# A transposing DMA in place of sixteen TensorE transposes in the feed-forwards that run beside attention

## The chip, the cores and the metric

The kernel runs on one core of one Trainium2 chip. The metric is the device time of one execution in microseconds (us); lower is better. Before the change the median of three runs is 2065.4 us (2061.41, 2065.40 and 2065.89). A forecast within 0.2% of the time before cannot be told from no change.

## What is computed

Four sequences (B = 4) of 512 tokens with 512 features pass through two layers, each with an attention part and a feed-forward part, all as residual updates scaled by the tanh of a gate:

```python
x = x + tanh(g_xattn[0]) * L0_xattn(ctx_512, layernorm(x))   # top-k adjacency, 153 of 512 kept
x = x + tanh(g_ffn[0])   * L0_ffn(layernorm(x))              # Hadamard, 8-bit, ternary weights
x = x + tanh(g_xattn[1]) * L1_xattn(layernorm(x), ctx_512)   # 16 heads, rotary, softmax
x = x + tanh(g_ffn[1])   * L1_ffn(layernorm(x))              # 8-bit, ternary weights
```

Both feed-forwards have the same inner shape. A row of 512 features goes up to 2048 by two products with ternary weights, silu(gate) times up gives the inner layer, and that layer is quantized before the product down to 512:

```python
def act_quant(x):
    scale = 127 / max(max(abs(x), axis=-1), 1e-5)
    return clip(round(x * scale), -128, 127) / scale
out = act_quant(inner) @ weight_quant(w_down).T        # inner: (tokens, 2048)
```

In layer 0 a Hadamard transform of length 2048 stands between the inner layer and act_quant. The rounded inner layer holds whole numbers, so it is kept in bfloat16 exactly.

## The kernel before

One core does everything. Tokens are cut into tiles of 128 rows on 128 partitions; a sequence has four (NT = 4). The work runs in three stretches:

- Opening, about the first 260 us: adjacency of sequence 0, ternary weights of layer 0, and feed0 of sequence 0 by itself. Here the flag alone[0] is True.
- The attention of layer 1 (generator attention, L877): 4 sequences times 8 pairs of heads. Between its steps the background is woven in: adjacency and feed0 of sequences 1 to 3, then the ternary weights of layer 1 (last_weights), then feed1 of sequences 0 to 2. A table of jobs (L985) with a cost and a due step decides how many background steps go between two attention steps. The flag is False here (L959).
- Close: feed1 of sequence 3 (L1015 on). The flag is True for that tile's own steps and False for what is left of feed1 of sequence 2, which is woven in (L1016 to L1020).

The order in which the source issues steps is only a first order. A scheduler in the compiler places every instruction in a fixed queue of its engine, by priorities and by its own estimates, and tile pools with fixed numbers of buffers decide what has to wait. Each engine, and the DMA queue of SyncE (SP), then takes its queue strictly in order: an instruction that waits holds up all behind it.

The quantized product down is in projected (L362). For one tile of 128 tokens:

1. DVE takes the row maximum (L377), scales and rounds with a magic number (L382), and unmagic (L205) writes q, 128 x 2048 bfloat16, on DVE (L210) when the flag is False, on ACT (L208) otherwise. q comes from a pool tag with one buffer.
2. turned (L197) turns q into zT, which has 16 blocks of 128 x 128: for each of four groups, four TensorE transposes into one PSUM bank (L202) and one ScalarE copy to SBUF (L203). zT has one buffer as well.
3. TensorE multiplies the 16 blocks with the ternary weights into pd (L399), with each block of zT as the loaded weight.
4. DVE adds pd to the residual (L569 in layer 0, L640 in layer 1).

The same helper turned is called with n = 1 for the 512 features at the entrance of each feed-forward (L541, L623), and with n = 4 for the inner layer (L393).

Background PSUM banks for turned come from bg_tr (L78): when the flag is False always from the background ring of two banks (tag bg), which it shares with the up and down products.

SP issues nearly all loads in one queue: the head weights wq (L731), wc (L734), wr (L736), the output weights om (L744) and the rotated keys kr (L800) of each pair, the raw weights of layer 1 (L222), the results (L642) and the spilled residuals (L581, L912). wc, wr and kr have one buffer and wq and om two, so most of these loads wait in SP's queue for TensorE to finish with the earlier contents.

Of the kernel before, what the change touches and what calls it, by code (L numbers as in the profile page):

```python
# [2 lines left out]

# [23 lines left out]
EPS = 1e-5  # L27
MAGIC = 12582912.0
GONE = -3.0e38
F8 = mybir.dt.float8e4  # L30


@with_exitstack
def flamingo_kernel(
# [9 lines left out]
    nc = tc.nc  # L44
# [20 lines left out]
    alone = [True]  # L65
# [12 lines left out]
    def bg_tr(name, dt=F32):  # L78
        if mine("tr", 4):
            return psb.tile([P, 4, P], dt, tag="bg", name=name)  # L80
        return pst.tile([P, 4, P], dt, tag="tr", name=name)
# [114 lines left out]

    def turned(src, dst, n, name):  # L197

        for k in range(n):
            pt = bg_tr(f"ptq_{name}_{k}", BF)  # L200
            for c in range(4):
                nc.tensor.transpose(pt[:, c, :], src[:, (4 * k + c) * P : (4 * k + c + 1) * P], identb)  # L202
            nc.scalar.copy(dst[:, 4 * k : 4 * k + 4, :], pt)  # L203
# [50 lines left out]
    def feed_weights(first, name):  # L254

        wa = bp.tile([P, NC, 2 * FF], F8, tag="wa", name=f"wa_{name}")
        wd = bp.tile([P, NF, D], F8, tag="wd", name=f"wd_{name}")
        down = (downT if first else outT).rearrange("(t c p) o -> t p c o", p=P, c=4)
# [103 lines left out]
    def projected(u, z, mul, wd, gd, last):  # L362
# [23 lines left out]
        else:  # L386
# [4 lines left out]
            yield 1.6  # L391
        zT = bp.tile([P, NF, P], BF, tag="zT", name=f"zT_{u}")
        turned(q, zT, 4, f"h{u}")  # L393
        col = small.tile([P, 1], F32, tag="cols", name=f"col_{u}")
        nc.vector.tensor_scalar(col, m, 1.0 / 127.0, gd, ALU.mult, ALU.mult)
# [14 lines left out]
    def adjacency(b):  # L410
# [16 lines left out]
        for two in range(0, NT, 2):  # L427
# [17 lines left out]
            for r in range(rounds):  # L445
# [5 lines left out]
                with tc.high_priority(offset=-FILL):  # L451
                    if r < rounds - 1:
                        for j in pair:
                            nc.vector.match_replace(works[j], m8[j], cur[j], GONE)  # L454
                            cur[j] = works[j]
# [44 lines left out]
    def feed0(b, w):  # L500
# [6 lines left out]
        for j in range(NT):  # L507
# [31 lines left out]
            unmagic(q, h)  # L539
            zq = bp.tile([P, NC, P], BF, tag="zq", name=f"zq_{u}", bufs=4)  # L540
            turned(q, zq, 1, f"a{u}")  # L541
            ready.append((zq, dg, du))
            yield 2.0
# [31 lines left out]
    def feed1(b, w, wn):  # L575
# [24 lines left out]
        for j in range(NT):  # L600
            u = f"g{b}_{j}"
            n = front_t(f"n_{u}")
            if quick:
                nc.scalar.activation(
                    n, xr[j], AF.Identity, bias=cc[:, j : j + 1], scale=ca[:, j : j + 1]
                )
                nc.vector.tensor_tensor(n, n, wn, ALU.mult)
            else:
                ln_tile(n, xr[j], j, mv, r)

                nc.vector.scalar_tensor_tensor(xr[j], n, tgf1, xr[j], ALU.mult, ALU.add)
                nc.vector.scalar_tensor_tensor(n, n, rr[:, j : j + 1], wn, ALU.mult, ALU.mult)
            amax = small.tile([P, 1], F32, tag="amax", name=f"amaxg_{u}")
            nc.vector.tensor_reduce(amax, n, AX.X, ALU.max, apply_absolute_value=True)
            yield 2.7
            m, sc = scales(amax, 1.0, f"g{u}")
            du = small.tile([P, 1], F32, tag="du", name=f"du_{u}", bufs=6)
            nc.vector.tensor_scalar(du, m, 1.0 / 127.0, s_gv, ALU.mult, ALU.mult)
            nc.vector.tensor_scalar(n, n, sc, MAGIC, ALU.mult, ALU.add)
            q = bp.tile([P, D], BF, tag="qa", name=f"qa_{u}")  # L620
            unmagic(q, n)
            zq = bp.tile([P, NC, P], BF, tag="zq", name=f"zq_{u}", bufs=4)
            turned(q, zq, 1, f"g{u}")  # L623
            ready.append((zq, du, du))
            yield 1.8
# [513 lines left out]
```

## Time and profile before

The profile is of one execution that took 2064.35 us, with 2062.6 us from its first to its last instruction.

| | busy us | share of the span | instructions |
|---|---|---|---|
| TensorE matmul (PE) | 1853.7 | 90% | 7274 |
| TensorE weight load (PEld) | 873.3 | 42% | 7274 |
| VectorE (DVE) | 1584.7 | 77% | 3233 |
| ScalarE (ACT) | 1176.6 | 57% | 1979 |
| GpSimd (POOL) | 333.1 | 16% | 316 |

The mean granted TensorE clock is 0.962 of full speed; the DMA engines moved 139.25 MB. Matmuls are pipelined, so the busy time of one is longer than the distance to the next: the distance is what the next matmul in the queue pays. In the profile's rows the letter f stands for feed0 and g for feed1, ptq for the PSUM tile of a transpose, and the number behind the tile is dropped. "idle before" is the time in which the engine stood still just ahead of the rows of the group.

### The profile page before, as it was taken

How to read it: one execution, taken by the hardware profiler on the slowest of the kernel's cores; microseconds unless marked ns; L12 is line 12 of the kernel's file. 1: busy time of each engine (PE TensorE's matmuls, PEld its weight loads, DVE VectorE, ACT ScalarE, POOL GpSimd, SP SyncE). 2: the span in 40 equal slices, each digit the busy share in tenths (PEclk: the TensorE clock that was granted, in tenths of full speed). 3: DMA queues.
4: the chain of work that ended last, by engine and by line, in shares of the span. 5: the costliest groups of instructions: out<-in, count | busy, mean ns of one | idle time of the engine just before them, and what ended most of it. 6: DMA issues, size and time to landing. Idle time of an engine off the chain costs nothing. (4 is left out here: it accounts for less than half of the span.)

```text
span 2062.6 us, 21752 instructions
## 1 busy us (share of the span) xinstructions
PE 1853.7 (90%) x7274; PEld 873.3 (42%) x7274; DVE 1584.7 (77%) x3233; ACT 1176.6 (57%) x1979; POOL 333.1 (16%) x316
## 2 busy tenths in 40 slices
PE   1268789999999999999999999999999999999898
PEld 0035434434544444445453444454444444444344
DVE  7989599986774999876769999767636755866775
ACT  6935454455544555455454554554899565567554
POOL 3010031122100221230011221300112210101000
PEclk6579899999999999999999999999999999999999
DMA  7451021210101222110012221101755111111000
GB/s 273 148 177 38 1 77 41 63 46 27 38 21 32 83 82 60 43 38 26 27 33 87 72 73 38 38 21 33 256 191 199 50 38 45 58 35 39 11 16 26
DMA packets 65633, 139.25 MB, mean 68 GB/s; under 512 B 7537, under 2 KB 18161, under 8 KB 62449
## 3 DMA queue, kind: packets, MB, share of 16 engines
q1 hardware_dynamic: 60048, 121.92, 18.7%
q0 software_dynamic: 4320, 14.16, 1.8%
q10 hardware_dynamic: 1152, 1.77, 0.2%
q8 instruction: 58, 0.95, 0.2%
q14 instruction: 55, 0.44, 0.1%
HBM read 117.90 MB, written 19.92 MB: 67 GB/s over the span
## 5 line engine op out<-in xcount | busy, mean ns | idle before, releaser
L793 POOL TENSOR_TENSOR ro<-ro,rs 128x512 f32<-128x512 f32 x192 | 252.7, 1319 | 1167.2 <-DVE rs L789 753.8
L834 ACT ACTIVATE pp<-pss,nm 128x512 f32<-128x512 f32 x256 | 175.1, 688 | 224.8 <-DVE nm L831 224.0
L764 PE MATMUL pqh<-hT,wq 128*128 128x512 f32 x512 | 239.6, 603 | 6.8 <-ACT pp L834 6.6
L853 PE MATMUL pc<-pT,kv 128*128 128x512 f32 x512 | 235.4, 598 | 0.7 <-ACT pT L846 0.6
L865 PE MATMUL po<-om,cxo 128*128 128x512 f32 x512 | 230.9, 597 | 0.0
L831 DVE TENSOR_REDUCE nm<-pss 128x1 f32<-128x512 f32 x256 | 167.6, 681 | 57.4 <-PE pss L826 56.5
L779 PE MATMUL pb<-qh,wc 128*128 128x512 f32 x384 | 191.1, 614 | 10.4 <-ACT qh L769 7.3
L449 DVE MAX8 m<-work 128x8 f32<-128x512 f32 x304 | 198.0, 680 | 0.6
L454 DVE MATCH_REPLACE8 work<-m,work 128x512 f32<-128x512 f32 x288 | 192.8, 674 | 0.1
L837 ACT ACTIVATE pp<-pp,rsm 128x512 f32<-128x512 f32 x256 | 178.9, 724 | 21.2 <-DVE rsm L836 20.9
L870 DVE SCALAR_TENSOR_TENSOR x<-po,gt,x 128x512 f32<-128x512 f32 x128 | 94.6, 744 | 92.4 <-PE po L865 91.9
L846 ACT COPY pT<-ppt 128x512 f32<-128x512 f32 x256 | 142.9, 592 | 28.9 <-PE ppt L845 28.8
L845 PEld LDWEIGHTS ppt<-ident,pp 128*128 128x128 f32 x1024 | 117.3, 141 | 86.0 <-issue 33.9
L845 PE MATMUL ppt<-ident,pp 128*128 128x128 f32 x1024 | 146.4, 277 | 6.7 <-ACT pT L846 3.5
L823 PE MATMUL pss<-kr,qr 64*128 64x512 f32 x256 | 144.3, 644 | 5.6 <-ACT pp L834 4.8
L764 PEld LDWEIGHTS pqh<-hT,wq 128*128 128x128 f32 x512 | 92.7, 191 | 125.4 <-issue 84.6
L826 PE MATMUL pss<-kr,qr 64*128 64x512 f32 x256 | 144.4, 645 | 0.5 <-DVE ro L787 0.5
L865 PEld LDWEIGHTS po<-om,cxo 128*128 128x128 f32 x512 | 93.7, 190 | 114.5 <-issue 98.1
L787 DVE TENSOR_TENSOR ro<-pb,cos_q 128x512 f32<-128x512 f32 x192 | 130.5, 680 | 11.0 <-PE pb L779 10.2
L853 PEld LDWEIGHTS pc<-pT,kv 128*128 128x128 f32 x512 | 92.7, 190 | 102.3 <-issue 88.7
L858 ACT COPY cxo<-pc 128x512 f32<-128x512 f32 x64 | 37.6, 587 | 135.7 <-PE pc L853 135.4
L750 PE MATMUL pr<-ro,wr 128*64 128x512 f32 x192 | 99.8, 613 | 14.3 <-POOL ro L793 12.2
(266 smaller groups left out, 3123.5 us busy)
## 6 DMA issues: line engine op xcount, KB each, us to landing
wq<-in_wqh SPq DMA_DIRECT2D x64, 256.0 KB, 2.7
om<-omd SPq DMA_DIRECT2D x64, 256.0 KB, 2.7
wc<-in_wkcq SPq DMA_DIRECT2D x32, 384.0 KB, 3.1
krd<-krs POOLq DMA_DIRECT2D x32, 256.0 KB, 2.4
kr<-krd SPq DMA_DIRECT2D x32, 256.0 KB, 2.7
sa_w1v<-in_gvT SPq DMA_DIRECT2D x8, 1024.0 KB, 5.3
sb_w1v<-in_gvT SPq DMA_DIRECT2D x8, 1024.0 KB, 5.5
wr<-in_wqr SPq DMA_DIRECT2D x32, 192.0 KB, 2.4
```

What stands on the lines that cost most here:

```text
L449: nc.vector.max(m8[j], cur[j])
L454: nc.vector.match_replace(works[j], m8[j], cur[j], GONE)
L764: nc.tensor.matmul(pq, self.wqs[i][:, c, :], hT[self.b][:, c, :], start=(c == 0), stop=(c == NC - 1),)
L779: nc.tensor.matmul(pb, self.wc[:, at : at + P], self.qhs[i if i < 2 else o], start=True, stop=True)
L793: nc.gpsimd.tensor_tensor(ro, ro, rs, ALU.add)
L826: nc.tensor.matmul(*args, start=True, stop=True)
L831: nc.vector.tensor_reduce(nm, pss[i], AX.X, ALU.max, negate=True)
L834: nc.scalar.activation(pp, pss[i], AF.Exp, bias=nm, accum_out=sm)
L837: nc.scalar.activation(pp, pp, AF.Copy, scale=rs)
L845: nc.tensor.transpose(pt[:, l, :], pp[:, l * P : (l + 1) * P], ident)
L853: nc.tensor.matmul(pc, kv[self.b][:, l, :], self.pT[i][:, l, :], start=(l == 0), stop=(l == NT - 1),)
L865: nc.tensor.matmul(po, self.cxo[i][:, j * P : (j + 1) * P], self.oms[i], start=(i == 0), stop=(i == 1),)
```

## The change

In turned, when n is above 1 and the flag is False, the loop of transposes and copies is not run; one transposing DMA is issued from SP, q to zT, and the function returns. Where the flag is True, and for n = 1, nothing changes.

```diff
-from contextlib import ExitStack
+from contextlib import ExitStack, nullcontext
...
+U16 = mybir.dt.uint16
 F8 = mybir.dt.float8e4
...
     def turned(src, dst, n, name):
 
+
+        if n > 1 and not alone[0]:
+            nc.sync.dma_start_transpose(dst, src)
+            return
         for k in range(n):
             pt = bg_tr(f"ptq_{name}_{k}", BF)
             for c in range(4):
```

The two new names at the top are not used. In the built kernel 24 transposing DMAs stand in SP's queue: four tiles each for sequences 1, 2 and 3 in feed0 and for sequences 0, 1 and 2 in feed1. TensorE's queue has 384 transposes fewer (of 7274 matmuls in the profile), and ScalarE's 96 copies fewer. The lines of the changed file lie five further down from this place on: the down product is L404, and the transposing DMA is L202.

## Prediction

> **What bounds the kernel now.** I read the page's busy rows first, then busy time by stage, because the change touches only the stretch with attention. The columns are length, then busy time of each engine with instruction counts, the granted TensorE clock, the DMA engines' share and GB/s.
>
> ```profile
> PE 1853.7 (90%) x7274; PEld 873.3 (42%) x7274; DVE 1584.7 (77%) x3233; ACT 1176.6 (57%) x1979; POOL 333.1 (16%) x316
> ```
> ```profile
> 520.00:940.00 420.00, 405.15 (x1537) 190.94 (x1536) 343.91 (x688) 215.00 (x410) 77.79 (x72) 0.99 0.16 49
> 940.00:1360.00 420.00, 404.75 (x1545) 189.92 (x1544) 345.03 (x693) 215.46 (x410) 79.76 (x72) 1.00 0.16 49
> 1360.00:1640.00 280.00, 265.72 (x1005) 124.60 (x1004) 177.16 (x332) 208.86 (x321) 45.04 (x33) 0.99 0.40 135
> ```
>
> TensorE is busy 96% of these stages at full clock, ACT about half, and the DMA engines 16%. TensorE time is what counts here, and it runs a fixed queue: an operand that comes late stops everything behind it. So I next looked at one tile's turn, in the timeline around 990 us (start, length, engine, line).
>
> ```profile
> 986.38 2.17 DVE L210 TENSOR_SCALAR q_f<-yb_f 128x2048 bf16<-128x2048 f32 x1
> ...
> 990.34 0.61 PE L202 MATMUL ptq_hf<-identb,q_f 128*128 128x128 bf16 x8
> ...
> 990.77 1.07 ACT L203 COPY zT_f<-ptq_hf 128x512 bf16<-128x512 bf16 x2 [1.52 <-PE ptq_hf L202]
> 990.79 1.08 PE L853 MATMUL pc<-pT,kv 128*128 128x512 f32 x2
> ...
> 991.70 0.61 PE L202 MATMUL ptq_hf<-identb,q_f 128*128 128x128 bf16 x8
> ...
> 993.07 3.62 PE L399 MATMUL pd_f<-wd_w,zT_f 128*128 128x512 fp8e4 x16
> ...
> 996.72 0.75 DVE L569 SCALAR_TENSOR_TENSOR x<-pd_f,col_f,x 128x512 f32<-128x512 f32 x1 [8.18 <-PE pd_f L399]
> ```
>
> Eight transposes take TensorE only from 990.34 to 990.79, 56 ns each, and lie among attention matmuls. pd starts 4.5 us after q ends at 988.55, with no gap. The last row says that DVE stands waiting for pd: a late pd is not absorbed there.
>
> **What it removes.** 24 tiles x 16 = 384 transposes. At 56 ns that is 21.5 us. The distances from each of them to the next matmul in the trace, added up, are 26.0 us, with a stall inside one group (3.1 us where others take 0.9). I take 25 us, all on the path, since TensorE is. It also removes 96 copies of 0.594 us, 57 us of ACT. ACT is not the bound, but in the waits of TensorE from 260 to 1960 us some 38 us end at ACT. A window of 420 us loses 16 copies or 9.5 us of its 215 us, 4.4%, which would be 1.7 us of those 38; since the copies stand close to other ACT work I take 3, between 0 and 10. Gain together: 28 us.
>
> **What it adds.** 24 transposing DMAs of 512 KB, each between q and pd. Call X the time from q's end to zT's landing. No such transfer is in the trace; the nearest rows are plain ones (KB each, median us to landing):
>
> ```profile
> wq<-in_wqh SPq DMA_DIRECT2D x64, 256.0 KB, 2.7
> sa_w1v<-in_gvT SPq DMA_DIRECT2D x8, 1024.0 KB, 5.3
> wk<-in_wkr SPq DMA_DIRECT2D x32, 64.0 KB, 1.9
> ```
>
> Interpolated, a plain 512 KB would take 3.6 us: the lower end. From the other side, 16 blocks have 2048 rows of 256 bytes, 128 per DMA engine. The trace's 512-byte packets take 28 ns, so a 256-byte one 14 to 28: 1.8 to 3.6 us, over about 1.7 us fixed (wk's 1.9 less its packets), so 3.5 to 5.3 us. To that comes SP's own time. The Trainium skill, "DMA: Bandwidth & Descriptors", part "trn3 B0 only", column for the generations before, gives 262,144 sequencer cycles for an SBUF-to-SBUF transpose of 8,192 tiles, 32 per tile, and 512 for a plain DMA. A plain issue holds SP 0.33 us in this trace. The built kernel's instruction names source tiles of 16 x 128, so 128 tiles, 4096 cycles, an estimated 2.6 us. If issue comes ahead of movement, X = 2.6 + 3.6 = 6.2 us; if they overlap fully, about 4.
>
> Two rules of the skill pull apart. The same page, "Latency and other measured facts", has transposing DMAs at 261 to 400 GB/s, which with the fixed 2 us of its "Anatomy of one DMA" makes X 3.3 to 4.0 us: the sum would be 20 us of gain or more. "VectorE: DVE Perf Modes", section "The three transpose paths", says to use TensorE for 128 x 128 if PSUM will do and has 1309 ns for a DMA block against 390 ns; sixteen blocks one after another are 21 us. The trace already corrects that page's TensorE figure to 56 ns in a stream, so blocks likely pipeline in a DMA too, and I do not take 21. X = 6.2 stands, with 4 and 10 as likely ends.
>
> **What covers X.** The scheduler's new order decides. I listed for each tile what stands in TensorE's new queue after q's end and before pd, with the trace's distances (an fp32 512-wide product 0.86 us, a 128-wide transpose 0.11). For the tile above six pc products stand there: 5.1 us. Cover in us, in order: feed0 of sequence 1: 3.6, 3.7, 2.4, 2.2; of 2: 3.7, 5.1, 5.2, 5.0; of 3: 3.7, 5.1, 5.2, 4.5; feed1 of sequence 0: 5.6, 6.1, 31, 4.6; of 1: 5.4, 29, 9.2, 2.8; of 2: 3.5, 18, 5.9, 9.1. Where X exceeds the cover, TensorE stops. The sum of the excesses is 6 us at X = 4, 18 at 5.2, 34 at 6.2, 108 at 10 and 343 at 21.
>
> A stop also costs clock. The stages around two gaps:
>
> ```profile
> 604.00:614.00 10.00, 7.29 (x34) 3.75 (x32) 9.85 (x12) 4.11 (x8) 0.00 (x0) 1.00 0.07 26
> 614.00:624.20 10.20, 10.16 (x30) 4.52 (x31) 8.69 (x14) 6.05 (x12) 3.44 (x2) 0.50 0.09 26
> ...
> 1494.70:1501.50 6.80, 5.30 (x19) 3.46 (x17) 0.61 (x2) 6.80 (x9) 0.00 (x0) 0.50 0.02 6
> ```
>
> After a TensorE gap of 2.5 us the clock was half for 10.2 us, after one of 1.8 us for 6.8 us: 5.1 and 3.4 us lost, mean 4.25. Gaps of 2.1 us (457) and 1.75 us (1764) cost nothing. The skill's "TensorE: Matmul & The Clock Gate", Part 1, halves the clock after an idle window of some 3.4 us. By that rule only the two stops above 3.4 us would pay at X = 6.2, 8.5 us; by the row, shorter ones pay every second time. I count 1 for stops over 3.4 us and a half for 1.8 to 3.4: at X = 6.2 two and six, so 5 x 4.25 = 21 us.
>
> **SP's queue.** The transpose waits for q there, and what stands behind waits too. In the new order these are the next wq, kr, wc, wr or om, a result, or for the last tile of sequence 3 four raw weights. Most of them were issued after q's end anyway (for the tile above om at 1014 us), because they wait for TensorE; wr for a pair that moves from 1709 to 1721 us is needed only after that pair's rope steps. SP time of 2.6 us x 24 thus costs nothing. If a load did stick it would cost up to 8 us once (the raw weights). Ahead of the transpose, the loads had left before q's end except for one result (1.5 us). q and zT have one buffer: the next q comes 7.4 us later at the closest, so this costs nothing up to that X. These edits: 0, ends 0 and 10.
>
> **Sum.** 2064.35 - 28 + 34 + 21 = 2091 us for the profiled execution; the median of the runs is 1 us above it, so 2092.
>
> **The rivals.**
> - *The DMA is as quick as a plain one, X about 4* (chance 0.31). For it speak the idle DMA engines and the 261 GB/s; against it 256-byte rows and the tiles that SP has to push. 2065.4 - 28 + 6 + 2 (half a clock drop) = 2045 us: faster. The point that decides is X = 5.4, where stops and clock (20.5 + 8.5) eat the 28.
> - *Likeliest: X of 5.5 to 8* (0.46): 2070 to 2168, with 2092 at 6.2.
> - *The blocks go one by one, X of 8 to 21* (0.18). For it speaks the 1309 ns a block; against it the streaming of everything else here. At X = 10: 108 + 81 - 28 = +161, 2226 us; at 21 +406, 2471 us. A late pd then also holds DVE's next q.
> - *Within 0.2%* (0.05): X between 5.2 and 5.5.
> - *That the change doesn't do what it says* is out: the 24 instructions stand in SP's queue and 384 transposes are gone from TensorE's.
>
> **The range.** 2042 is X = 4 with a little more relief of ACT, 2240 is X a little over 10. Below lies 0.07, above 0.13. Faster by over 0.2% 0.31, within 0.05, slower 0.64.
>
> **What would show it.** In the profile after: the DMA issue row of zT with its median to landing, near 6 us; the weight load of pd (L404) or its matmul with idle time ended by the DMA of zT, some 34 us in all and longest in sequence 1 and the last tile of feed1 of sequence 1; more slices with a clock under 9; TensorE's busy time lower by the 384 transposes; ACT busy some 57 us less. I am wrong if zT lands in under 5 us (then faster), if L404 waits for nothing although it does not, or if loads (wq, kr, sa_w1v) turn up as what TensorE waits for.

## The result and the profile after

The changed kernel takes 2050.2 us, median of six runs (2047.06 to 2055.69), against 2065.12 us for six runs of the kernel before: ratio 0.9933, with a 95% interval of 0.9917 to 0.995. That is 0.7% faster where 1.3% slower was forecast. The profiled execution took 2050.43 us, with 2048.7 us from first to last instruction; that of before took 2064.35 us.

The page after, its busy rows, and the groups of the transposing DMA and of the wait for it. "SPq" is SyncE issuing; the three numbers are the shortest, median and longest ns that one issue holds the queue, and "to landing" counts from the start of the issue.

```profile
PE 1834.1 (90%) x6890; PEld 854.8 (42%) x6890; DVE 1584.0 (77%) x3233; ACT 1128.1 (55%) x1883; POOL 337.0 (16%) x316
```
```profile
L202 SPq DMA_TRANSPOSE zT_f<-q_f x12: 1712/2435/3136, 527.8 to 1469.3; - x12
...
  DVE x L574: 62.9, 12
```
```profile
L202 SPq DMA_TRANSPOSE zT_g<-q_g x12: 1693/1932/3351, 1684.4 to 1999.0; - x12
...
DMA to landing us min/median/max: 4.3/4.3/5.7
```

TensorE has 384 instructions and 19.6 us less, ACT 96 copies and 48.5 us less (the lengths of the copies themselves fall by 58, near the forecast's 57, but in part they overlap their neighbours). DVE waits for pd_f 62.9 us where the same group waited 49.4 before: the product down is later, as foreseen, but little. The forecast put the landing near 6 us; it is 4.3 from the start of the issue.

Before, TensorE did not stand ahead of pd. Its groups (busy us, mean ns of one, idle before):

```profile
L399 PE MATMUL pd_g<-wd_w,zT_g 128*128 128x512 fp8e4 x256 | 60.1, 389 | 0.2 <-ACT zT_g L203 0.2
L399 PE MATMUL pd_f<-wd_w,zT_f 128*128 128x512 fp8e4 x256 | 58.8, 383 | 0.0
```

The waits of TensorE after, from 260 to 1960 us (total us, times, longest):

```profile
PE pr L755 <- POOL ro L798: 12.5, 12, 1.4
PE pb L784 <- ACT qh L774: 8.2, 10, 1.3
PE pd_f L404 <- DMA zT_f<-q_f: 5.5, 8, 1.1
...
PE pd_g L404 <- DMA zT_g<-q_g: 4.3, 4, 1.9
```

The wait stands where it was expected, at the product down, and it is 9.8 us, not 34. The same tile that the prediction showed, in the timeline after:

```profile
987.94 5.42 PE L858 MATMUL pc<-pT,kv 128*128 128x512 f32 x12
988.08 0.33 SPq L741 DMA_DIRECT2D wr<-in_wqr  x1
988.51 1.81 SPq L202 DMA_TRANSPOSE zT_f<-q_f  x1
993.20 3.62 PE L404 MATMUL pd_f<-wd_w,zT_f 128*128 128x512 fp8e4 x16
...
996.85 0.75 DVE L574 SCALAR_TENSOR_TENSOR x<-pd_f,col_f,x 128x512 f32<-128x512 f32 x1 [8.89 <-PE pd_f L404]
```

q ends at 987.96; wr's load is ahead of the transpose in SP's queue and costs 0.55 us; zT lands at 993.04, 4.53 us after the issue began, while twelve pc matmuls, the forecast's six products, fill TensorE. pd starts 0.16 us later and TensorE has not stopped. The longest stop is this one, in the first tile of feed1 of sequence 2, where 5.7 us passed between issue and landing:

```profile
1945.59 3.63 PE L404 MATMUL pd_g<-wd_w,zT_g 128*128 128x512 fp8e4 x16 [1.95 <-DMA zT_g<-q_g]
```

And the stages around it show that the clock stayed full:

```profile
1938.00:1944.00 6.00, 5.64 (x21) 2.29 (x19) 4.45 (x6) 1.78 (x3) 0.00 (x0) 1.00 0.76 87
1944.00:1952.00 8.00, 6.41 (x27) 3.01 (x28) 4.94 (x9) 1.27 (x2) 0.00 (x0) 1.00 0.23 43
```

**Where the 13.9 us are.** I added up the distances from the start of each matmul to the start of the next, from 250 us on. The last matmul ends at 2044.5 us instead of 2058.0, 13.5 us earlier, and the first 250 us are unchanged (the sums begin at 250.2 and 250.1). The transposes of the inner layer take 26.2 us less (20.9 to 6.9 in feed1, 12.2 to 0 in feed0). Where zT came last, the distance to pd less the usual distance of the instruction ahead sums to 12.8 us. -26.2 + 12.8 is -13.4. That this is so near the 13.5 is in part luck: one more stop of 1.8 us ahead of pd, at 1971 us, is ended by ScalarE (sg_g) 17 us after zT landed, and other small gains and losses cancel it. The time at half clock after 238 us went from 30.6 to 33.1 us, 1.3 us lost.

### The profile page after: what moved, and what is told of

Same layout as the page of the kernel before. It is cut to its first block, busy times and chain, and to the rows that moved or that the text cites. A ratio compares the mean times of both kernels' runs of the same rounds, so it can differ in the third digit from the quotient of the medians.

```text
span 2048.7 us, 20950 instructions
## 1 busy us (share of the span) xinstructions
PE 1834.1 (90%) x6890; PEld 854.8 (42%) x6890; DVE 1584.0 (77%) x3233; ACT 1128.1 (55%) x1883; POOL 337.0 (16%) x316
## 5 line engine op out<-in xcount | busy, mean ns | idle before, releaser
L784 PE MATMUL pb<-qh,wc 128*128 128x512 f32 x384 | 190.9, 614 | 13.1 <-ACT qh L774 8.2
```

The source lines that it names most:

```text
L784: nc.tensor.matmul(pb, self.wc[:, at : at + P], self.qhs[i if i < 2 else o], start=True, stop=True)
```

## The experiments

Line numbers of the variants are up to four further down. Each group of runs had the kernel before on the same chip: its medians were 2063.97 us (experiments 1 to 4), 2063.31 (halves, the later product and its control, feed0_only) and 2063.52 (the others). Ratios are against that.

**1. TensorE's slots back, the DMA stays (pe_back).** After the DMA the sixteen transposes run again, on zT, into background PSUM that nothing reads; no copies.

```diff
             nc.sync.dma_start_transpose(dst, src)
+            for k in range(n):
+                pt = bg_tr(f"ptq_{name}_{k}", BF)
+                for c in range(4):
+                    nc.tensor.transpose(pt[:, c, :], dst[:, 4 * k + c, :], identb)
```

> Each transposing DMA stays, and TensorE gets its 16 transposes per tile back, reading zT after it has landed, into PSUM banks that nobody reads; no copies on ScalarE. Theory A (what was won is the 384 slots of TensorE, 25 us, less the waits for zT): about 22 to 26 us above the changed kernel, 2072 to 2076 us, slower than before by some 8 us, because the waits stay. Theory B (what was won is the 96 copies of ScalarE): within 5 us of the changed kernel.

Measured: 2081.57 us, ratio 1.0078 (1.0066 to 1.0091), against 0.9933 for the changed kernel: 30 us more (24 against its repeat in experiment 7). TensorE's waits for zT stay, 10.0 us, now ahead of the transposes. The forecast's 25 us for these slots account for most of the 30. The half clock after 238 us, 44.1 us instead of 33.1, would be 5.5 more, but the repeat of the changed kernel has 46.2. What the change gains are the slots of TensorE, and the theory that puts the gain in ScalarE's copies falls.

**2. ACT's copies back, the DMA stays (act_back).** Four copies of 128x512 per tile from q into a bank of the background ring, unread.

```diff
             nc.sync.dma_start_transpose(dst, src)
+            for k in range(n):
+                jt = bg_ps(f"jt_{name}_{k}")
+                nc.scalar.copy(jt, src[:, 512 * k : 512 * (k + 1)])
```

> Each transposing DMA stays, and ScalarE gets four copies of 128x512 per tile back (from q into a background PSUM bank that nobody reads). Theory A: 0 to 5 us above the changed kernel (2050 to 2055), as ScalarE is not the bound. Theory B: about 14 us above it, the whole gain gone.

Measured: 2058.74 us, ratio 0.997 (0.996 to 0.9981), about 8 us above the changed kernel (2 above its repeat). The group of pd in feed1 says what most of that is:

```profile
L407 PE MATMUL pd_g<-wd_w,zT_g 128*128 128x512 fp8e4 x256 | 65.4, 413 | 5.7 <-ACT jt_hg L205 5.2 <-DMA zT_g<-q_g 0.4
```

5.2 us are pd waiting for the bank that a copy holds, 4.6 of it once at 1981 us, when the attention is over; the copies of before stood ahead of pd anyway. The remaining 3 us fit the term of 3 in the sum, but one run with such a side effect, and with the repeat this much slower, does not fix it.

**3. A plain DMA in place of the transposing one (plain_copy).** The turning is left out: zT gets q's rows as they are, so that the time is that of the removal plus a plain transfer.

```diff
-            nc.sync.dma_start_transpose(dst, src)
+            nc.sync.dma_start(dst.rearrange("p c q -> p (c q)"), src)
```

> A plain DMA of the same 512 KB from q to zT in place of the transposing one, so that the turning itself is left out of the computation in these 24 tiles. It measures what the turning costs over a plain transfer. Theory A (TensorE waits some 13 us for zT, as zT lands 4.3 us after issue): a plain transfer lands in 3.0 to 3.6 us, the waits shrink to 3 to 8 us, 2040 to 2046 us. Theory C (the waits are hidden by other work and cost nothing): 2050 us as with the transposing one.

Measured: 2038.48 us, ratio 0.988 (0.9865 to 0.9895), 25.5 us below before. Its DMA rows (KB each, median us to landing) and the group of pd in feed0:

```profile
zT_f<-q_f SPq DMA_DIRECT2D x12, 512.0 KB, 3.1
zT_g<-q_g SPq DMA_DIRECT2D x12, 512.0 KB, 2.9
```
```profile
L404 PE MATMUL pd_f<-wd_w,zT_f 128*128 128x512 fp8e4 x256 | 58.6, 383 | 0.5 <-DMA zT_f<-q_f 0.4
```

With the operand some 1.4 us earlier TensorE stops for 1.1 us in all, and the gain of 25.5 us comes within 1.4 of the 28 that the forecast gave to the removal less these stops. Turning in flight therefore costs about 12 us (16 by the ratio of the repeat), and the 12.8 us of stops of the changed kernel are enough to explain the 12.

**4. A first quarter moved twice (quarter_twice).** This makes X longer by a known step. The whole waits until the quarter has landed, since both write the same blocks.

```diff
+            nc.sync.dma_start_transpose(dst[:, 0:4, :], src[:, 0:512])
             nc.sync.dma_start_transpose(dst, src)
```

> The first quarter of q is turned by a DMA of its own ahead of the whole, into the same place, so that zT lands later, about 6 to 7 us after q if the two run one after the other. It puts the changed kernel where the prediction had placed it. Theory A (excess over the cover stops TensorE, and stops over 1.8 us cost clock): the new order covers 5 to 8 us, excess 12 to 26 us in place of 13, plus 2 to 17 us of clock, 2053 to 2080 us. Theory C (waits cost nothing): 2050 us. If the two overlap in the DMA engines zT lands under 5.5 us and the time stays at 2045 to 2052 us.

Measured: 2075.38 us, ratio 1.005 (1.0037 to 1.0063): slower than before. The first tile of feed0 of sequence 1 in its timeline:

```profile
526.45 1.29 SPq L202 DMA_TRANSPOSE zT_f<-q_f  x1
529.39 1.90 SPq L203 DMA_TRANSPOSE zT_f<-q_f  x1
532.32 0.34 SPq L737 DMA_DIRECT2D wq<-in_wqh  x1
533.82 3.61 PE L405 MATMUL pd_f<-wd_w,zT_f 128*128 128x512 fp8e4 x16 [1.54 <-DMA zT_f<-q_f]
```

X is 6.7 us and more here, 7.5 on average and up to 9.7 in one tile; the stops add up to 20.2 us and the half clock to 46.9. The forecast's sum with these is 2064.35 - 28 + 20.2 + 8.2 = 2064.8 us. The profiled execution took 11.6 us more: 5.0 of them are longer waits of TensorE for ScalarE ahead of pss, and the rest I cannot place. At 7.5 us the forecast's table of covers gives 59 us of stops; the scheduler put other work ahead of pd in this kernel, so the table is not tested by it. What the run shows is the sign: with an X above the 6.2 us of the forecast this change is a loss, of 0.5%.

**5. Two halves (halves).** The same turning in two transfers of eight blocks; pd starts on the first half.

```diff
-            nc.sync.dma_start_transpose(dst, src)
+            for k in range(0, n, 2):
+                nc.sync.dma_start_transpose(dst[:, 4 * k : 4 * k + 8, :], src[:, 512 * k : 512 * (k + 2)])
```

> The transposing DMA of a tile is cut into two, each for eight of the sixteen blocks, so that the down product can begin on the first half. From the two sizes measured (128 KB lands 2.4 us after issue, 512 KB 4.3) the first half should land at about 3.0 us, and the second about 1.4 us later, while the product takes 1.7 us for the first eight blocks. Theory A (TensorE waits for zT, and that wait is the whole cost): the waits go from 13 us to about 5, 2040 to 2045 us, between the changed kernel and the plain copy. Theory D (what costs is the work of turning in SP's queue and the DMA engines, not the wait): no gain, 2050 us or above, as SP has twice the instructions.

Measured: 2041.74 us, ratio 0.9895 (0.988 to 0.9911). In the waits of the whole span:

```profile
PE pd_f L405 <- DMA zT_f<-q_f: 4.0, 7, 1.0
...
PE pd_g L405 <- DMA zT_g<-q_g: 1.9, 4, 0.7
```

A half holds SP 1.24 us and lands 3.2 us after its issue began, so pd can start about a microsecond earlier and the second half lands while it runs. Some 4.5 of the 10.4 us of waits in the whole span are gone, and the ratio is lower by 0.4 points (8 us; against the repeat of the changed kernel in experiment 7 by 0.65). What is not waits I cannot place.

**6. A later product, and the same order without the DMA (later_product, later_product_before).** To let the scheduler put more work ahead of pd, its matmuls got a lower priority; the control gives the kernel before the same.

```diff
-        for c in range(NF):
-            nc.tensor.matmul(
+        with nullcontext() if alone[0] else tc.high_priority(offset=-240):
+            for c in range(NF):
+                nc.tensor.matmul(
```

> The changed kernel with the matmuls of the down product at a lower priority for the scheduler (240 below) wherever the transposing DMA is used, so that over 6 us of other work stands ahead of each product in TensorE's queue. Theory A: no product waits for zT any more, and if the new order costs nothing by itself 2036 to 2042 us. What speaks against it: the product now trickles in between other matmuls and holds one of the two background PSUM banks for longer, which may cost as much; the control shows that.

> Control: the kernel before, with TensorE transposes and copies, and the same lower priority of the down product. Theory A: the kernel before had no wait at the product, so the order brings nothing here, 2060 to 2075 us; the difference to the run with the transposing DMA and the same priority is the gain without the waits, 24 to 30 us.

Measured: 2142.98 us, 1.0388 (1.0372 to 1.0405), and the control 2124.94 us, 1.0302 (1.0286 to 1.0317). A miss: the order alone costs some 62 us.

```profile
PE pd_f L405 <- DMA zT_f<-q_f: 34.7, 4, 12.9
```

In some of feed0's tiles pd starts 16 to 27 us after q, far more than X needs; but at the last tile of each sequence TensorE had run everything placed ahead of pd before q was even rounded, and stood 10.6 to 12.9 us. In the control it stands at the same three places 6.3 to 6.5 us, for q alone. zT has one buffer, and one transpose in feed1 was issued 35 us after its q. Of the 18 us between the two, 15 are more half clock in the profiled executions (108.3 against 78.3 us). This tells nothing about the cover as such; it shows that this shift of priority does not buy it.

**7. One feed-forward alone, and the changed kernel again (feed0_only, feed1_only, changed_again).** The edit of feed0_only; feed1_only has "hg" in its place, and changed_again is the changed kernel as it is.

```diff
-        if n > 1 and not alone[0]:
+        if n > 1 and not alone[0] and name.startswith("hf"):
```

> The transposing DMA for the twelve tiles of feed0 only; feed1 as before. By the sums of the traces feed0 saves 12 us of TensorE slots and waits 7 us, feed1 saves 13 and waits 6, so each should bring about half of the 14 us: 2056 to 2060 us.

> The counterpart of the run with feed0 only, which brought 0.3%: the transposing DMA for the twelve tiles of feed1 only. If the two parts add up, 2055 to 2059 us, 0.3 to 0.45% below the kernel before.

> The changed kernel itself once more, on the same chip as the three other runs of this call, so that they can be compared directly: 2047 to 2056 us, ratio to the kernel before 0.993.

Measured: feed0 alone 2057.51 us, 0.9969 (0.9959 to 0.998); feed1 alone 2055.26 us, 0.9961 (0.9947 to 0.9974); the changed kernel once more, beside feed1_only, 2056.19 us, 0.996 (0.9946 to 0.9974). The parts gain 0.31% and 0.39%, together 0.7%, the first gain of the whole. But the repeat of the whole gives 0.4%, no more than feed1 alone on the same chip, so that the parts add up is not shown. The intervals of the repeat and of the first runs just overlap, and the change is faster in both. The stops are alike in the two profiles (13.1 and 12.8 us where zT came last); the half clock is not, 46.2 and 33.1 us, which is 6.5 us of time from one and the same program. So a difference of 0.3% between variants of different groups is not to be read.

**8. Halves, and the entrance too (halves_entry).** The 512 features at the entrance of the feed-forwards (n = 1, zq) go by DMA as well.

```diff
-        if n > 1 and not alone[0]:
+        if not alone[0]:
```

> The inner layer turned in two halves, and also the 512 features at the entrance of each feed-forward beside attention (n = 1, 24 tiles of 128 KB) by a transposing DMA. That takes another 96 transposes (5.4 us of TensorE slots) and 24 copies off. A 128 KB transpose lands 2.4 us after issue, and the products that use it mostly stand more than 5 us later in the queue. Theory A (slots of TensorE less waits): 4 to 7 us below the run with halves, 2034 to 2039 us, with no wait of the up products (L307 of the changed file) for zq. Theory D (more instructions in SP's queue cost): 2042 us or above.

Measured: 2063.16 us, 0.9999 (0.9991 to 1.0008). A miss, and a large one: another 96 transposes leave TensorE and the whole gain is lost. TensorE's waits in this kernel:

```profile
PE pn_f L529 <- POOL n_f L526: 19.0, 24, 2.1
...
PE pr L757 <- POOL ro L800: 13.6, 15, 1.5
...
PE pg_g L309 <- ACT sg_g L314: 10.3, 7, 2.8
```

and in halves:

```profile
PE pr L756 <- POOL ro L799: 9.7, 10, 1.4
...
PE pn_f L528 <- POOL n_f L525: 5.1, 7, 2.1
PE pg_g L308 <- ACT sg_g L313: 4.3, 6, 1.5
```

None of them is a wait for zq. TensorE's gaps after 250 us sum to 114.9 us instead of 87.3. In halves, the turns of one tile's entrance stand ahead of the next tile's pn_f, which starts 7 to 9 us after that of the tile before; without them the distance is 5 to 7 us, pn_f stands close behind GpSimd's Hadamard steps, and TensorE, which takes its queue in order, waits for GpSimd 24 times instead of 7. This reading rests on the waits of two traces; no run separates the new order from the new DMAs.

**9. Halves in all 32 tiles (halves_everywhere).** The opening and the close use the DMA too.

```diff
-        if n > 1 and not alone[0]:
+        if n > 1:
```

> The inner layer turned in two halves by DMA in all 32 tiles, also where a feed-forward runs alone (feed0 of sequence 0, feed1 of sequence 3). There TensorE is not full, so the 128 transposes it saves there are worth little, and what counts is the time from q to zT: 3.3 us for the first half by DMA against about 2.7 us in feed0 and 6 to 9 us in feed1 of sequence 3 by TensorE and ScalarE in the trace before. Theory A: within 6 us of the run with halves, 2036 to 2048 us, the opening a little later and the close a little earlier.

Measured: 2033.31 us, ratio 0.9853 (0.984 to 0.9866), the quickest of all: 1.5% below before. The last 110 us in windows (columns as in the prediction), of this kernel and then of halves:

```profile
1960.00:2070.00 110.00, 59.00 (x272) 25.62 (x270) 50.87 (x99) 26.87 (x35) 0.00 (x0) 0.98 0.20 46
```
```profile
1960.00:2070.00 110.00, 70.22 (x360) 32.23 (x359) 56.59 (x116) 41.63 (x60) 0.00 (x0) 0.96 0.09 27
```

At 1960 us 11.2 us less of TensorE work is left and 14.8 us less of ACT's. 7.1 us of it are the close's 64 transposes; the rest was done earlier: by 260 us DVE has run 18 instructions more than in halves, although TensorE waits for zT there, 13.1 us in all and up to 6.9 at a time (in halves its transposes wait there for q instead, 14.9 us and up to 6.8). In the opening TensorE is not what bounds the time (102 of the 130 us up to 260 are busy in halves, as many as DVE's 103), so those waits cost little.

## Why the prediction was wrong

It was wrong in sign, by one step and what hangs on it. The step is the line **X = 2.6 + 3.6 = 6.2 us**, which puts SP's issue and a whole landing one after the other. The likeliest case was built on it. What came lies nearest to the rival with X about 4 (2045 us, chance 0.31), but not for that rival's reason: the DMA is not as quick as a plain one, 4.3 us to landing against 2.9. The forecast's own sign of being wrong, zT landing in under 5 us, came true.

- **X.** Measured from q's end to zT's landing, over the 24 tiles: mean 4.7 us, from 4.3 to 5.7. Of its two branches the forecast built on the one in which issue comes ahead of movement, and that is what failed: they overlap. For the second tile of feed0 in sequence 1, issued at 567.98 us, the trace has this (columns of the windows as in the prediction; packets count where they start, so the DMA share can pass 1):

```profile
567.98 1.71 SPq L202 DMA_TRANSPOSE zT_f<-q_f  x1
567.98:569.14 1.16, 1.16 (x4) 0.44 (x4) 0.00 (x0) 0.00 (x0) 0.00 (x0) 1.00 0.00 0
569.14:569.69 0.55, 0.55 (x3) 0.31 (x2) 0.00 (x0) 0.39 (x1) 0.00 (x0) 1.00 0.96 190
569.69:571.80 2.11, 2.11 (x6) 0.60 (x4) 0.00 (x0) 1.48 (x2) 0.00 (x0) 1.00 1.05 199
571.80:572.27 0.47, 0.04 (x1) 0.00 (x0) 0.00 (x0) 0.00 (x0) 0.00 (x0) 1.00 0.00 0
```

  SP issues until 569.69, but the packets move from 569.14: the first comes 1.2 us after the start of the issue, the 2048 packets take 2.6 us, and the landing follows 0.5 us after the last. Of the 24, 14 run like this one. The forecast had this sum in its hands: its count of packets, 1.8 to 3.6 us over 1.7 us fixed, is 2.6 + 1.7 = 4.3 us as measured, and needed no time of SP on top.
- **The two terms themselves.** Both were too large as well. The 2.6 us on SP, an estimate from the sequencer cycles that the Trainium skill gives in "DMA: Bandwidth & Descriptors", are 1.7 to 3.4 us, mean 2.2. The 3.6 us was interpolated between transfers from HBM; the plain SBUF-to-SBUF transfer of the same 512 KB in plain_copy lands in 2.9 us (median). Its packets move for 1.4 us, those of the transposing one for 2.6. Seven of the 24 issues took 2.8 us and more, and these landings 4.4 to 5.1; what held them up stays open.
- **The excess of 34 us.** The table of covers was right in its total: it gave 6 us at X = 4 and 18 at 5.2, which is 13 at 4.7, and 12.8 are measured. Tile by tile it was not: for the last two tiles of feed0 in sequence 1 it gives 4.7 us with their measured X, where 0.6 came, and nothing for several tiles that stopped 0.6 to 0.8 us. That these errors cancel is luck.
- **The clock's 21 us.** Measured 1.3, and 7.8 in the profile of the repeat. At this X only one stop for zT is above 1.8 us (2.1 us, with the clock at 1.00 around it). The forecast weighed a stop by its length, and the traces show that the length alone does not decide. In all fourteen traces the granted clock changes only on a grid of 3.41 us, so that half-clock stretches last 3.4, 6.8 or 10.2 us and so on. From 238 us on, without the last two steps of each trace, there are 58 steps at full clock in which the profile has TensorE busy less than 0.40 of the step, and each was followed by half clock; between 0.40 and 0.55 it was 24 of 73, above that 7 of 7154. Two stops ahead of pd in quarter_twice, of 2.4 us up to 955.0 and of 2.5 us up to 1463.9, with the grid steps around them:

```profile
951.10:954.50 3.40, 1.52 (x9) 0.69 (x6) 1.99 (x5) 3.01 (x8) 0.00 (x0) 1.00 0.89 165
954.50:957.90 3.40, 2.92 (x14) 1.39 (x15) 0.00 (x0) 1.52 (x2) 0.00 (x0) 1.00 0.17 66
1459.70:1463.10 3.40, 1.12 (x2) 0.29 (x2) 3.40 (x6) 1.70 (x3) 0.00 (x0) 1.00 1.11 281
1463.10:1473.30 10.20, 9.40 (x21) 3.31 (x22) 3.98 (x7) 2.83 (x6) 3.47 (x2) 0.50 0.41 130
```

  The first left TensorE busy 0.45 of its step and cost nothing, the second 0.33, and half clock followed for 10.2 us. So where a stop falls on the grid, and what else is idle in the same step, counts with its length. An idle window of 3.4 us, as "TensorE: Matmul & The Clock Gate", Part 1, has it, was not needed.
- **The 28 us of gain.** Right: 26.2 us of slots in the trace, 25.5 us for plain_copy, 30 us for pe_back with its clock. ACT's part of 3 is neither shown nor excluded.
- **SP's queue at no cost.** Right: beside attention no load became what TensorE waits for. The transposes did wait behind a load's issue now and then, 0.55 us for the tile above, which is the most. One came 0.93 us after its q, when pd of the tile before had just done with zT's one buffer: I had taken the buffer as free at the landing, but it is free when pd has read it.
- **The two rules of the skill that pulled apart.** The quick one, an estimate from transposing DMAs at 261 GB/s and more with 2 us fixed in "DMA: Bandwidth & Descriptors", made X 3.3 to 4.0 and 20 us of gain; measured are 4.7 and 14. The packets of the tile above moved at 190 to 199 GB/s, and that page gives the 2 us for transfers issued from GpSimd, not from SP. The slow one, 1309 ns a block in "VectorE: DVE Perf Modes", would have needed 21 us for sixteen blocks, which took 4.3. The blocks are not done one by one. That page's advice to use TensorE, which stands in its "Rules for kernel authors", did not hold here, where TensorE is the busy engine.
- **A reading of the rows.** ACT at about half and the DMA engines at 16% is right for the first two stages shown; in the third ACT is busy 75% and the DMA engines 40%. No term of the sum rests on it.

With the measured X, stops and clock the forecast's own sum is 2064.35 - 28 + 12.8 + 1.3 = 2050.4 us; the profiled execution took 2050.43. That it agrees this closely is luck: the terms are known to a microsecond or two, the slots measured 26.2 us and not 25, ACT's 3 us are not shown, and the stop of 1.8 us for ScalarE is not in the sum. For the repeat the same sum gives 2057.3 us, and its profiled execution took 2054.45.

## What to carry to other kernels

When a fixed queue must wait for a new transfer, the sign hangs on that transfer's latency less the work already queued ahead of its reader; list that cover per tile, find the latency at which gain and stops cancel, and then spend the effort on the latency. Count each part of it once: a time to landing already contains its issue, packets can move while the queue still issues, and a transfer from another memory is not the nearest row merely because its size is near. If pieces can be read as they land, split the transfer, and look at the new order of the other engines' queues before taking more instructions out: halves gained, and taking out the entrance as well gave all of it back.

## What the runs showed of the hardware

- A transposing DMA from SBUF to SBUF, bfloat16, by size (median us on SP's queue, median from start of issue to landing): 128 KB 1.19 and 2.4; 256 KB 1.24 to 1.32 and 3.2; 512 KB 1.96 and 4.3, with seven of the 24 issues at 2.8 us and more. The plain 512 KB: 0.47 and 2.9.
- Inside an undisturbed 512 KB transfer: the transposing one has its first packet 1.2 us after the start of the issue, 2048 packets of 256 bytes in 2.6 us (200 GB/s), and lands 0.5 us after the last; the plain one its first packet after 1.1 us, 128 packets of 4096 bytes in 1.4 us (362 GB/s), and lands 0.4 us after the last.
- The granted clock changes only on a grid of 3.41 us in every trace, and each of the 58 steps with TensorE busy under 0.40 was followed by half clock, as told above.
- Two stops of 10.6 us ahead of pd_f in later_product had the clock at half from about 3 us after their start, for 10 and 14 us in all, most of which lay inside the stop.
